# Slack instead of program order in the planner of a four-layer hybrid kernel

## The chip, the cores and the metric

The kernel runs on one core of a Trainium2 chip. The metric is device time in microseconds: before the change the median of three runs is 7542.12 us (7540.26 to 7549.51). Five engines work side by side, each through its own queue in order: TensorE (PE, matrix products), VectorE (DVE), ScalarE (ACT), GpSimd (POOL), and SyncE (SP), whose queue only starts transfers here. An instruction that isn't ready holds up everything behind it on its engine.

## The reference

The input `x` is 4 images of 96 channels, 64 by 64, in fp32. Four layers follow one another:

- Layer 0: two Mamba blocks over the 4096 pixels of an image as a sequence. In each: layer norm, a projection to 2 x 192 channels, a causal convolution of 4 taps, SiLU, and then a selective scan with 16 states per channel. Last a pooled gate, a 1x1 fusion, batch norm over all images, and the residual.
- Layer 1: group norm, then two 2-D selective-scan blocks ("ss2d"), each with a 3x3 depthwise convolution and a scan with 8 states in four directions (row by row, column by column, and both reversed), layer norm and a gate.
- Layer 2: a Fourier mixing layer over the tokens and a feed-forward layer quantized to a small float format.
- Layer 3: attention without softmax, and another such feed-forward layer.

The part that fills both planned stages is the scan:

```python
def step(h, inp):
    a, bu, c = inp                 # a = exp(delta * A), bu = delta * B * x
    h = a * h + bu
    return (h, jnp.einsum('bkdn,bkn->bkd', h, c))
```

## The kernel before

The kernel has three stages, one after the other: `stage_mamba` (layer 0), `stage_ss2d` (layer 1) and `stage_tokens` (layers 2 and 3). The third is written in the order in which it is issued. In the first two the code only records its operations, with a planner (`class Plan`, line 281), and `pl.run(tc)` at the stage's end issues them in the order that the planner chose. Every planned instruction carries line 466 in the profile, the line in `Plan.run` that issues it, so the profile's groups are told apart by tile names.

**The scan.** Both stages cut the sequence into turns of 1024 tokens. A turn is split into scan units: one unit is 128 rows (states times channels) by 1024 tokens. A mamba turn has 24 units and there are 32 turns; an ss2d turn has 6 units, and 128 turns make eight blocks of 96 units: 768 units in each stage. A block is one of the two ss2d layers on one image. For one unit:

- SP loads `sc_d`, the step `delta` spread over the states, from the DRAM tile `dd`; ACT turns it into the decay with Exp.
- In two units of three ("spread" units) PE makes `s`, `delta * x` spread over the rows, in PSUM (`Scan.inputs`), and DVE multiplies it by `B` (`bc`). In the third unit SP loads it as `sc_u` from `ud`, POOL multiplies it by `B`, and ACT writes the decay to `s`.
- DVE runs the scan (`TENSOR_TENSOR_SCAN`, 1024 steps); ACT copies the last column to `carry` for the next turn.
- POOL multiplies by `C` into `sc_h` (`Scan.outputs`), and PE sums over the states into `y` (`Scan.reduce`).

Besides, each turn has to be prepared: projections, convolution, `delta`, their way through DRAM (`dd`, `ud`, and in ss2d `bcd`, `bc_in` and `bc_stack` for `C`); and finished: gate, output projection. In ss2d a whole block is also convolved ahead (nine taps, 576 matmuls over the eight blocks, `mm<-xp,w_conv` in the profile) and normed behind. These side works are recorded between the units, step by step, by `Work.pace`; in ss2d the finish of the block before and the preparation of the block after are one such work, spread over the units of the running block (`between`, due near its end).

Buffers: `s` has two PSUM tiles, `y` one, `sc_d` six, `sc_u` three (two in ss2d), `sc_h` seven (five in ss2d). These are rings whose turn is fixed as the code is recorded. Only the two `mm` PSUM tiles are handed out by the planner itself (`Hold`).

**The planner.** `Plan.add` records an operation with a fixed cost from `Plan.cost` (its engine and its columns), and `Plan.touch` adds the operations it must come after. `Plan.order` (line 384) then plays the schedule forward. Every engine has a clock; the engine that can start first takes, among its ready operations, the one with the lowest `index`, the place in which the code recorded it. An engine never waits for a better operation while it has a ready one. Table switches on ACT cost `SWITCH`, a change of matmul form `TURN`, a hand-over between engines `SYNC`. An operation that needs an `mm` tile when none is left is parked; a freed tile wakes the one parked operation with the lowest index.

Of the kernel before, what the change touches and what calls it, by code (L numbers as in the profile page):

```python
# [280 lines left out]
class Plan:  # L281
# [2 lines left out]


    TABLE = {AF.Exp: "exp", AF.Silu: "silu", AF.Softplus: "softplus"}
    SWITCH, TURN, SYNC = 1283.0, 100.0, 100.0

    def __init__(self, nc):
        self.nc, self.ops, self.seen, self.open = nc, [], {}, None  # L290
# [91 lines left out]
        return 60.0  # L382

    def order(self):
        free = {}
        for hold in {h for op in self.ops for h in op.holds.values()}:

            first = hold.ops[0]
            first.after |= {by for op in hold.ops for by in op.after if by.index < first.index}
            for op in hold.ops[1:]:  # L390
                op.after.add(first)
        for op in self.ops:
            op.left = len(op.after)
            for by in op.after:
                by.then.append(op)
            for hold in op.holds.values():
                hold.left = len(hold.ops)
                free.setdefault(id(hold.ring), ([(0.0, t) for t in hold.ring], []))
        names = ("tensor", "vector", "scalar", "gpsimd", "sync")
        wait, can = {n: [] for n in names}, {n: [] for n in names}  # L400
        clock = dict.fromkeys(names, 0.0)
        table, form, link, out = None, None, 0.0, []
        for op in self.ops:
            if not op.left:
                heappush(wait[op.engine], (0.0, op.index, op))
        while len(out) < len(self.ops):
            at, name = min(
                (clock[n] if can[n] else max(clock[n], wait[n][0][0]), n) for n in names if can[n] or wait[n]
            )
            while wait[name] and wait[name][0][0] <= at:  # L410
                _, index, op = heappop(wait[name])
                heappush(can[name], (index, op))
            _, op = heappop(can[name])
            new = [h for h in op.holds.values() if h.buffer is None]
            if new:
                assert len(new) == 1
                buffers, parked = free[id(new[0].ring)]
                if not buffers:
                    heappush(parked, (op.index, op))
                    continue  # L420
                since = min(b[0] for b in buffers)
                if since > at:
                    heappush(wait[name], (since, op.index, op))
                    continue
                n = min(range(len(buffers)), key=lambda n: buffers[n][0])
                new[0].buffer = buffers.pop(n)[1]
            cost = op.cost
            if op.form:
                cost += self.TURN * (op.form != form)
                form = op.form  # L430
            if op.table and op.table != table:
                cost += self.SWITCH
                table = op.table
            op.start = at
            clock[name] = op.end = at + cost
            if name == "sync":
                link = max(link, at + 2200.0) + op.land - 2200.0
                op.end = link
            out.append(op)
            for hold in op.holds.values():  # L440
                hold.left -= 1
                if not hold.left:
                    buffers, parked = free[id(hold.ring)]
                    end = max(o.end for o in hold.ops) + self.SYNC
                    buffers.append((end, hold.buffer))
                    if parked:
                        _, o = heappop(parked)
                        heappush(wait[o.engine], (end, o.index, o))
            for o in op.then:
                o.ready = max(o.ready, op.end + (self.SYNC if o.engine != name else 0.0))  # L450
                o.left -= 1
                if not o.left:
                    heappush(wait[o.engine], (o.ready, o.index, o))
        return out

    def run(self, tc):
# [1229 lines left out]
```

## Time and profile before

| | |
|---|---|
| median of three runs | 7542.12 us |
| the profiled execution | 7571.38 us, span 7569.0 us |
| instructions | 84054 |
| PE, DVE, ACT, POOL busy over the span | 88%, 76%, 59%, 76% |
| mean clock granted to PE | 0.905 |
| scan on DVE, mean of one | 2.3 us (x1536) |
| multiply on POOL, mean of one | 2.36 us (x2048) |
| table loads on ACT | 499, 1283 ns each |
| HBM traffic | 1238.48 MB read, 174.06 MB written |

From the first scan to the last, mamba takes 72 to 2876 us and ss2d 2985 to 6170 us; the tokens stage begins at about 6230. A busy share is an average over a stage; what an engine waits for is in the lists of waits, where a line names the waiting engine and tile, what released it, and then total us, times, and the longest. A group's line has the busy time and the mean of one in ns, and after the second bar the idle time of the engine just before the group's instructions. Matmuls overlap and their ends are modelled, so that PE's busy time is not a measure of how much more it could do.

### The profile page before, as it was taken

The numbers are of one execution on the slowest core, as the hardware profiler recorded it, in microseconds if no ns is written. First come the engines' busy times: TensorE is split into PE (matmuls) and PEld (weight loads), VectorE is DVE, ScalarE is ACT, GpSimd is POOL, SyncE is SP. The second block draws the span as 40 slices with busy tenths as digits, with TensorE's granted clock in tenths as the row PEclk, the third lists the DMA queues.
The fourth block names the chain that finished last, engine by engine and source line by source line (L and its number), as shares of the span: only waits on it lengthen the run. The fifth ranks groups of instructions, "written<-read, shape, count | busy, mean of one in ns | idle before, by whom it ended". The sixth has DMA issues, their size and how long they took to land. (4 is left out here: it accounts for less than half of the span.)

```text
span 7569.0 us, 84054 instructions
## 1 busy us (share of the span) xinstructions
PE 6648.2 (88%) x28616; PEld 2867.8 (38%) x28616; DVE 5764.4 (76%) x4491; ACT 4499.9 (59%) x6656; POOL 5765.3 (76%) x2836
## 2 busy tenths in 40 slices
PE   8888888988888877989898898989898868999997
PEld 3322233323323222323232333323232228778784
DVE  6989988988898985898887878788888863344342
ACT  4655555555555544777777676677777644445442
POOL 6989988989998985889897978889898870232323
PEclk9999999999999998999898898989898888889897
DMA  7988988988888886999898989899999960000000
GB/s 192 239 224 232 230 216 220 239 222 226 227 235 217 222 224 168 233 241 230 223 234 222 244 218 241 215 230 232 230 238 238 236 176 22 1 18 5 15 9 9
DMA packets 448078, 1418.13 MB, mean 187 GB/s; under 512 B 81626, under 2 KB 91539, under 8 KB 445600
## 3 DMA queue, kind: packets, MB, share of 16 engines
q1 hardware_dynamic: 447648, 1412.76, 72.7%
q8 instruction: 225, 3.69, 0.2%
q14 instruction: 205, 1.68, 0.1%
HBM read 1238.48 MB, written 174.06 MB: 187 GB/s over the span
## 5 line engine op out<-in xcount | busy, mean ns | idle before, releaser
L466 POOL TENSOR_TENSOR sc_h<-sc_d,bc 128x1024 f32<-128x1024 f32 x1024 | 2406.9, 2360 | 394.8 <-DVE sc_d L466 186.0
L466 DVE TENSOR_TENSOR_SCAN sc_d<-sc_d,carry,s 128x1024 f32<-128x1024 f32 x768 | 1799.7, 2344 | 74.7 <-ACT sc_d L466 18.2
L466 DVE TENSOR_TENSOR s<-s,bc 128x1024 f32<-128x1024 f32 x1024 | 1248.7, 1220 | 505.3 <-PE s L466 500.2
L466 PE MATMUL s<-du,c_sel 96*128 96x512 f32 x2048 | 1124.0, 678 | 226.6 <-DVE sc_d L466 127.3
L466 ACT ACTIVATE sc_d<-sc_d,w_alog 128x1024 f32<-128x1024 f32 x1024 | 1165.7, 1144 | 257.4 <-DMA sc_d<-dd 253.7
L466 POOL TENSOR_TENSOR sc_h<-sc_u,bc 128x1024 f32<-128x1024 f32 x512 | 1208.0, 2359 | 112.2 <-PE y L466 73.1
L466 POOL TENSOR_TENSOR sc_u<-sc_u,bc 128x1024 f32<-128x1024 f32 x512 | 1208.2, 2360 | 100.9 <-DMA sc_u<-ud 87.6
L466 PE MATMUL y<-sc_h,c_red 128*32 128x512 f32 x6144 | 1094.5, 656 | 87.2 <-POOL sc_h L466 83.2
L466 DVE TENSOR_TENSOR_SCAN sc_u<-s,carry,sc_u 128x1024 f32<-128x1024 f32 x384 | 895.2, 2331 | 36.7 <-ACT s L466 17.5
L466 PE MATMUL s<-du,c_selp 128*128 128x512 f32 x1408 | 729.8, 647 | 112.3 <-DVE sc_d L466 108.8
L466 PEld LDWEIGHTS s<-du,c_sel 96*128 96x128 f32 x2048 | 396.2, 208 | 869.8 <-issue 427.7
L466 ACT ACTIVATE s<-sc_d,w_alog 128x1024 f32<-128x1024 f32 x512 | 570.8, 1115 | 240.7 <-DVE sc_d L466 155.7
L466 ACT ACT_TABLE_LOAD x499 | 640.2, 1283 | 8.7
L466 DVE TENSOR_TENSOR_SCAN sc_d<-sc_d,s 128x1024 f32<-128x1024 f32 x256 | 583.1, 2282 | 23.0 <-ACT sc_d L466 6.2
L508 POOL TENSOR_TENSOR ln_rs<-ln_rs_e,mhalf 128x4 f32<-128x4 f32 x128 | 134.9, 1056 | 582.9 <-DVE ln_rs_e L506 581.2
L466 PE MATMUL mm<-xp,w_conv 96*96 96x512 f32 x1152 | 528.7, 600 | 4.6 <-ACT bc L466 2.2
L466 PEld LDWEIGHTS y<-sc_h,c_red 128*32 128x32 f32 x6144 | 197.7, 114 | 848.9 <-issue 529.7
L466 ACT COPY carry<-sc_d 128x1 f32<-128x1 f32 x768 | 142.8, 186 | 565.5 <-DVE sc_d L466 564.0
L466 PEld LDWEIGHTS s<-du,c_selp 128*128 128x128 f32 x1408 | 263.2, 201 | 539.4 <-issue 274.7
L466 PE MATMUL mm<-hn,conv_w 97*64 97x512 f32 (+1 forms) x1024 | 368.8, 615 | 22.5 <-DVE hn L466 22.5
L466 PEld LDWEIGHTS mm<-xp,w_conv 96*96 96x96 f32 x1152 | 185.3, 164 | 310.1 <-issue 295.5
L466 DVE TENSOR_TENSOR_SCAN sc_u<-s,sc_u 128x1024 f32<-128x1024 f32 x128 | 290.7, 2271 | 14.1 <-ACT s L466 7.9
(211 smaller groups left out, 9343.6 us busy)
## 6 DMA issues: line engine op xcount, KB each, us to landing
sc_d<-dd SPq DMA_DIRECT2D x1536, 512.0 KB
sc_u<-ud SPq DMA_DIRECT2D x512, 512.0 KB
bc<-dd SPq DMA_DIRECT2D x128, 512.0 KB
dd<-delta SPq DMA_DIRECT2D x128, 448.0 KB
bc<-bcd SPq DMA_DIRECT2D x64, 512.0 KB
ud<-du SPq DMA_DIRECT2D x192, 128.0 KB
dd<-delta SPq DMA_DIRECT2D x32, 512.0 KB
ud<-du SPq DMA_DIRECT2D x32, 512.0 KB
```

Of the source, the lines that this page charges most:

```text
L466: getattr(getattr(self.nc, op.engine), method)(*a, **kw)
L508: nc.gpsimd.tensor_tensor(rs, ve, self.mhalf[:p, 0:n], ALU.pow)
```

## The change

The planner no longer ranks by `index` alone. It makes six rounds. In each it plays the schedule forward by the ranks it has (`schedule`, in the first round by `index`), notes the end that its own costs give, and then plays the schedule backward from that end (`push_back`): each engine takes the operations from the last to the first, those that ended latest first, as late as what follows them allows. An operation's start in this backward schedule, the latest that it found, becomes its rank for the next round, so that an operation with much slack ranks late. The round with the earliest end by the planner's costs is issued, with the `mm` tiles that it chose. A smaller change goes with it: a freed `mm` tile now wakes all operations parked for one, not only the first.

```diff
-    SWITCH, TURN, SYNC = 1283.0, 100.0, 100.0
+    SWITCH, TURN, SYNC, ROUNDS = 1283.0, 100.0, 100.0, 6
...
         for op in self.ops:
-            op.left = len(op.after)
+            op.rank = op.index
             for by in op.after:
                 by.then.append(op)
+        best = None
+        for _ in range(self.ROUNDS):
+            out = self.schedule()
+            end = max(op.end for op in out)
+            if best is None or end < best[0]:
+                best = end, out, {op: list(op.holds.values()) and [h.buffer for h in op.holds.values()] for op in out}
+            self.push_back(out, end)
+        for op in best[1]:
+            for h, buffer in zip(op.holds.values(), best[2][op] or ()):
+                h.buffer = buffer
+        return best[1]
+
+    def push_back(self, out, end):
+        names = ("tensor", "vector", "scalar", "gpsimd", "sync")
+        wait, can = {n: [] for n in names}, {n: [] for n in names}
+        clock = dict.fromkeys(names, 0.0)
+        for op in out:
+            op.left, op.ready = len(op.then), 0.0
+            op.length = op.end - op.start
+            if not op.left:
+                heappush(wait[op.engine], (0.0, -op.end, op.index, op))
+        for _ in out:
+            at, name = min(
+                (clock[n] if can[n] else max(clock[n], wait[n][0][0]), n) for n in names if can[n] or wait[n]
+            )
+            while wait[name] and wait[name][0][0] <= at:
+                _, rank, index, op = heappop(wait[name])
+                heappush(can[name], (rank, index, op))
+            _, _, op = heappop(can[name])
+            done = at + op.length
+            clock[name] = at + op.cost if name == "sync" else done
+            op.rank = end - done
+            for o in op.after:
+                o.ready = max(o.ready, done + (self.SYNC if o.engine != name else 0.0))
+                o.left -= 1
+                if not o.left:
+                    heappush(wait[o.engine], (o.ready, -o.end, o.index, o))
+
+    def schedule(self):
...
             if not op.left:
-                heappush(wait[op.engine], (0.0, op.index, op))
+                heappush(wait[op.engine], (0.0, op.rank, op.index, op))
...
                 if not buffers:
-                    heappush(parked, (op.index, op))
+                    parked.append(op)
                     continue
...
-                    if parked:
-                        _, o = heappop(parked)
-                        heappush(wait[o.engine], (end, o.index, o))
+                    for o in parked:
+                        heappush(wait[o.engine], (end, o.rank, o.index, o))
+                    parked.clear()
...
                 if not o.left:
-                    heappush(wait[o.engine], (o.ready, o.index, o))
+                    heappush(wait[o.engine], (o.ready, o.rank, o.index, o))
```

Nothing else changes: the recorded operations, their costs, the rings and the third stage are the same.

More of the change, by code (lines that the diff above doesn't have):

```diff
@@ L384, in order @@
     def order(self):
-        free = {}
         for hold in {h for op in self.ops for h in op.holds.values()}:
@@ L392, in order @@
         for op in self.ops:
-            op.left = len(op.after)
+            op.rank = op.index
             for by in op.after:
                 by.then.append(op)
+        best = None
[35 more added lines that the diff above has]
+    def schedule(self):
+        free = {}
+        for op in self.ops:
+            op.left, op.ready = len(op.after), 0.0
             for hold in op.holds.values():
-                hold.left = len(hold.ops)
+                hold.left, hold.buffer = len(hold.ops), None
                 free.setdefault(id(hold.ring), ([(0.0, t) for t in hold.ring], []))
@@ L410, in order @@
             while wait[name] and wait[name][0][0] <= at:
-                _, index, op = heappop(wait[name])
-                heappush(can[name], (index, op))
-            _, op = heappop(can[name])
+                _, rank, index, op = heappop(wait[name])
+                heappush(can[name], (rank, index, op))
+            _, _, op = heappop(can[name])
             new = [h for h in op.holds.values() if h.buffer is None]
@@ L418, in order @@
                 if not buffers:
-                    heappush(parked, (op.index, op))
+                    parked.append(op)
                     continue
-                since = min(b[0] for b in buffers)
-                if since > at:
-                    heappush(wait[name], (since, op.index, op))
+                buffers.sort(key=lambda b: b[0])
+                if buffers[0][0] > at:
+                    heappush(wait[name], (buffers[0][0], op.rank, op.index, op))
                     continue
-                n = min(range(len(buffers)), key=lambda n: buffers[n][0])
-                new[0].buffer = buffers.pop(n)[1]
+                new[0].buffer = buffers.pop(0)[1]
             cost = op.cost
```

## The prediction

> **What bounds the kernel now.** I read the page's 40 slices first, for stages; then busy times in windows, one for each stage and four of 100 us inside the second; then, in the worst of these, the groups of instructions and who waited for whom; last the same list of waits over the whole run.
>
> The slices. PE, DVE, POOL and the clock granted to PE, 189 us to a digit. DVE and POOL stand at 8 and 9 up to slice 33 and then drop: that end is the third stage, which has no planner.
>
> ```profile
> PE   8888888988888877989898898989898868999997
> ...
> DVE  6989988988898985898887878788888863344342
> ...
> POOL 6989988989998985889897978889898870232323
> PEclk9999999999999998999898898989898888889897
> ```
>
> Busy times by window: start:end, length, then PE, PE's weight loads, DVE, ACT and POOL, each with its count, then clock, DMA share and GB/s. The first three rows are the stages (mamba, ss2d, tokens).
>
> ```profile
> 0.00:2850.00 2850.00, 2494.04 (x8578) 848.55 (x8580) 2503.82 (x1588) 1588.87 (x2162) 2519.46 (x1113) 0.93 0.87 224
> 2850.00:6230.00 3380.00, 2921.96 (x8568) 1010.35 (x8564) 2777.36 (x1953) 2324.80 (x3459) 2894.77 (x1332) 0.90 0.88 225
> 6230.00:7569.00 1339.00, 1232.20 (x11473) 1008.93 (x11472) 483.21 (x952) 586.23 (x1035) 351.10 (x392) 0.86 0.05 14
> ```
>
> ```profile
> 4100.00:4200.00 100.00, 70.99 (x180) 20.92 (x182) 73.32 (x47) 60.21 (x94) 76.60 (x35) 0.78 0.85 213
> 4400.00:4500.00 100.00, 99.92 (x292) 34.75 (x291) 74.53 (x47) 69.00 (x97) 74.90 (x34) 1.00 0.74 195
> 4500.00:4600.00 100.00, 72.77 (x200) 22.29 (x200) 84.90 (x54) 80.58 (x118) 84.34 (x37) 0.88 0.98 254
> 4800.00:4900.00 100.00, 99.49 (x280) 34.24 (x279) 77.10 (x49) 70.69 (x102) 85.00 (x37) 1.00 0.83 221
> ```
>
> In both planned stages three engines share the load almost evenly: in mamba 88% each, in ss2d PE 86%, POOL 86%, DVE 82%. Neither stage has one bound; each loses what the three lose by being heavy at different times. In mamba they are heavy together. In ss2d they take turns: PE runs at 99% in one stretch and at 71 to 73% in the next, some 400 us apart, which is one block of 96 scan units. Inside 4400:4500:
>
> ```profile
> L466 PE MATMUL mm<-xp,w_conv 96*96 96x512 f32 x115 | 50.9, 594 | 0.0
> POOL sc_h L466 <- PE y L466: 19.2, 7, 4.6
> DVE s L466 <- PE s L466: 16.5, 8, 3.8
> ```
>
> Half of PE's time there is the convolution of the next block, never idle before it, while the scan's multiply on DVE waits for its `s` and POOL waits for `y`. Over the whole run:
>
> ```profile
> DVE s L466 <- PE s L466: 500.2, 311, 15.6
> POOL sc_h L466 <- DVE sc_d L466: 186.0, 153, 11.9
> ```
>
> The 500 us of DVE waiting for `s` is the largest wait of a well-loaded engine in the planned stages, and what an order can change.
>
> **What the Trainium skill says.** "Perfetto Trace Analysis", Optimization Strategy: a kernel with several regimes may gain by "interleaving those regimes". The windows above agree that ss2d has two. The same page, Identifying the Most-Contended Engine, warns that busy PE is not PE at its limit; the trace agrees (weight loads fill 30% of ss2d where matmuls fill 86%), so I weigh POOL and DVE as much as PE. "TensorE: Matmul & The Clock Gate", Architectural detail: ACT and DVE are strict FIFO; so an instruction that stands too early blocks all behind it. Its Part 1 has the clock halved after an idle window; here the clock is 0.78 where PE is 71% busy and 1.00 where it is 99.9%.
>
> **The change part by part.** No instruction of the planned work is added or removed; `order` at line 384 hands out the same operations in another order, with other buffers for the `mm` tiles. What follows is counted from the two kernels' orders as built.
>
> 1. It does act. In mamba the fourth of the six rounds is issued, in ss2d the second. Mean shift of an operation in its engine's queue: PE 12 and 14 places of 2,472 and 2,824, ACT 9 and 10, DVE 6 and 2, POOL 2 and 1.
>
> 2. PE's load in ss2d is spread. I counted the convolution's 576 matmuls between every 24 scan units: before, the eight blocks have pairs such as 63 then 9 or 51 then 21; after, 34 and 38, or 34 and 27. Then I gave every operation its mean from the trace's groups (scan 2.33, POOL multiply 2.36, DVE multiply 1.22, PE matmuls scaled so that ss2d sums to 2,919 us beside the trace's 2,922), put each engine's operations to the scan units they stand between, and summed over stretches the busiest engine's load. By 24 units: 3,229 us before, 3,101 after, minus 128 (in one block PE 128 then 78 before, 97 then 104 after, against POOL's 85). By 12 units minus 120; by 6 minus 98; by 8 minus 64; by 4 plus 8. Which length is right depends on how far engines drift apart: `s` has two buffers, `sc_h` five, loads run five units ahead, so 6 to 12. Bounds: plus 8 to minus 128; I take minus 80. A second way gives nearly that: mamba, whose PE load is even, needs 2,804 us from its first scan to its last for 2,535 us of POOL work; at this ratio ss2d's 2,817 us of POOL work in the same window take 3,116 us, 69 less than its 3,185.
>
> 3. The same sum in mamba changes by between plus 6 and minus 13 at 6 to 24 units. But there too the longest stretches of other PE work between two `s` shrink: those over 10 us fall from 24 to 11 (ss2d: 27 to 12), what lies beyond 8 us from 161 to 118 us. Bounds 0 and minus 43; DVE's queue and POOL's fill part of it, so I take minus 20.
>
> 4. Against it: PE changes between output heights 169 times more (1,014 to 1,104; 1,357 to 1,436). No row prices a change. From 0, since PE has some 10% idle, to 0.5 us each, the excess of a weight load's wait of 0.79 us after a change over the 0.24 us without one: 85 us. I take 10. Four more table loads at 1,283 ns are 5 us on ACT, which is 69% busy in ss2d: nothing, and 5 us without that cover.
>
> 5. Loads get later. SP is one queue in order, and it waits now (for POOL's `sc_h` alone, 1,705 us). I took for every load of `sc_d` the latest work that it or a DMA ahead of it in SP's queue waits for, and counted units from there to its own scan. In ss2d before, 4 loads have a lead of one unit or less and 11 of two; after, 18 and 32, behind the small `bcd` and `bc_in` transfers. Mamba hardly changes. A unit takes 4.15 us (3,185 us of scans over 768). The first load is issued at 64.5 us and its decay starts at 72.2: at most 7.7 us, then 1.15 us of decay. A lead of one is late by up to 4.7 us, of two by 0.6: 17 x 4.7 + 32 x 0.6 = 98, less the same sum of before, 21: 77 us at most. The start's 7.7 us has a queue of other loads in it, so I take 15.
>
> 6. The stages' ends: the last 8 units of ss2d stand in the same order, the 100 us between the stages and the drain at 6170:6230 keep their chains. Nothing; no cover is needed. The tokens stage is untouched.
>
> Sum: minus 80, minus 20, plus 10, plus 15: minus 75 us. The profiled execution took 7,571.4 us around a span of 7,569.0, 29 us above the median of 7,542.1; I take the difference from each alike: 7,496 profiled, 7,467 as median.
>
> **The rivals.** *Already absorbed.* The time of 24 scan units in ss2d is read from the starts of the scans: the stretch of the heaviest PE load (115) took 98 us and a light one (70) 112. Buffers carry some of the peak over, and the sum by 4 units says no gain. Then minus 40 to plus 15: 7,530. Against it: 16.5 and 19.2 us of waits in a single 100 us.
>
> *More than that.* If the flatter PE lets DVE's 500 us of waits fall by half, both stages gain: 7,290. For it: PE's clock sags in exactly the light stretches (0.78) and would do so less. Against it: the second way of part 2, which ends at minus 69 for ss2d.
>
> *Slower: late loads.* In ss2d's queue on SP a `bcd` write that waits for ACT stands ahead of the next `sc_d`; its decay comes late, the scan behind it holds DVE, and POOL starves. Price: the full 77 us of part 5, with part 4 at 85 us, against a gain of 100: 7,604. It decides from where the 49 late loads cost more than 100 / 49 = 2 us each. Against it: DVE waited for ACT's `sc_d` only 21 us in ss2d before. For it: POOL already waits 58 us there on loads of `sc_u`.
>
> *No change at all*, because the first round is issued, is excluded by part 1.
>
> **How the numbers follow.** The likeliest, minus 40 to minus 160 (7,382 to 7,502), has 0.54. More than that 0.13; absorbed 0.16, of which 0.07 within 0.2%, about what a measurement of this kernel can tell from no change, and 0.09 a little faster; late loads 0.17. Faster 0.54 + 0.13 + 0.09 = 0.76, same 0.07, slower 0.17. The range takes in the absorbed case, half of the late loads, and half of the large gain: 7,340 to 7,590.
>
> **What would show it.** Right: no stretch of ss2d with PE at 99% beside one at 72%; DVE's waits for `s` well under 500 us; from first scan to last some 3,110 us in ss2d (now 3,185) and 2,785 in mamba (now 2,804). Part 5 shows as ACT's waits for DMA before `sc_d`, now 254 us. Wrong: DVE's waits for `s` gone to ACT's decay, or the same length of ss2d with an even PE. The order was planned on fixed costs; where a real duration differs, a queue that stands tighter passes each delay on, and that could undo all of it.

## The result

The changed kernel takes 7565.74 us (median of 20 runs, 7542.01 to 7599.86) beside 7546.77 us before (20 runs, 7527.69 to 7566.74): ratio 1.0027, 95% interval 1.0015 to 1.0038. It is slower by some 20 us. The forecast was 75 us less; the time lies in the range, on the wrong side of no change.

The profiled execution took 7586.82 us around a span of 7585.0. The stages, from the starts of the scans in the two traces:

| us | before | after |
|---|---|---|
| mamba, first scan to last | 2802.8 | 2809.8 |
| last mamba scan to first ss2d scan | 109.3 | 105.5 |
| ss2d, first scan to last | 3183.8 | 3209.4 |
| last scan to the end | 1399.7 | 1384.9 |

So ss2d has the largest difference of this pair, 25.6 us, more than the 16.0 us between the two spans; mamba has 7.0 us more, and the last row, most of it the tokens stage in which nothing changed, has 14.8 us less. One execution of each is not enough to give ss2d's loss a size: the order of before took 3,184 us here and 3,167 in a kernel below, the changed one 3,209 here and 3,180 below. The verdict is that of the timed runs; the traces are read for what moved inside.

The page's slices after, PE, DVE, POOL and PE's clock, to be held against those of before:

```profile
PE   8899898988888987799989898889898777999997
...
DVE  6889988997999885887988788888888863344343
...
POOL 5989998998999885888998888889898961232323
PEclk9999999999999987898999899989899878889897
```

Busy times by window, as before: the first two stages, then the same four stretches of ss2d (start:end, length, then PE, weight loads, DVE, ACT, POOL, clock, DMA share, GB/s):

```profile
0.00:2850.00 2850.00, 2504.73 (x8555) 848.35 (x8558) 2494.16 (x1578) 1584.39 (x2157) 2511.03 (x1109) 0.92 0.87 223
2850.00:6230.00 3380.00, 2918.61 (x8491) 1012.42 (x8486) 2789.54 (x1930) 2330.73 (x3453) 2888.10 (x1323) 0.90 0.89 224
```

```profile
4100.00:4200.00 100.00, 85.33 (x235) 28.25 (x236) 81.69 (x55) 80.06 (x119) 82.04 (x36) 0.91 0.97 244
4400.00:4500.00 100.00, 97.76 (x277) 33.22 (x277) 90.50 (x57) 78.20 (x113) 86.18 (x38) 0.96 0.87 218
4500.00:4600.00 100.00, 89.17 (x250) 28.95 (x249) 80.78 (x51) 77.78 (x113) 82.00 (x36) 0.94 0.97 232
4800.00:4900.00 100.00, 95.70 (x281) 32.66 (x282) 88.17 (x55) 76.63 (x110) 89.13 (x39) 1.00 0.94 233
```

PE is even now: 85, 98, 89 and 96% where it was 71, 100, 73 and 99%. What the change was expected to do to PE it did, and the stage is no shorter.

The list of waits over the whole run, the line that was shown of before (there 500.2) and two that changed with it (before: 253.7 and 155.7):

```profile
DVE s L508 <- PE s L508: 439.0, 308, 10.5
...
ACT sc_d L508 <- DMA sc_d<-dd: 327.2, 239, 7.5
ACT s L508 <- DVE sc_d L508: 315.2, 145, 8.5
```

Now DVE's waits inside ss2d alone (2985 to 6170 us: total, times, longest), first before, then after:

```profile
DVE s L466 <- PE s L466: 289.0, 170, 15.6
DVE bc_in L466 <- ACT mm L466: 41.6, 33, 3.5
...
DVE sc_u L466 <- POOL sc_u L466: 22.0, 25, 2.7
DVE sc_d L466 <- ACT sc_d L466: 21.1, 13, 4.1
```

```profile
DVE s L508 <- PE s L508: 224.3, 155, 5.6
DVE sc_d L508 <- ACT sc_d L508: 62.0, 33, 6.5
DVE bc_in L508 <- ACT mm L508: 53.8, 55, 3.1
DVE sc_u L508 <- POOL sc_u L508: 36.1, 28, 5.8
```

The wait for `s` is 65 us less (15.6 of it is one wait ahead of the first scan of before). The waits for the decay, for a copy of ACT and for POOL's `sc_u` are 41, 12 and 14 us more. DVE waits as long as before, for others.

**Where in a turn.** I took the step from each scan's start to the next, and put DVE's busy and idle time into it. A turn of ss2d has six units, so by their places in DVE's queue 127 steps lead into the first unit of a turn and 640 stay inside one. (Busy and idle add up to some 50 us more than the steps, since records of neighbours overlap.)

| ss2d, us | into a turn: sum | busy | idle | inside: sum | busy | idle |
|---|---|---|---|---|---|---|
| before | 487.8 | 417.8 | 73.3 | 2696.0 | 2370.2 | 373.6 |
| after | 592.2 | 454.3 | 142.0 | 2617.3 | 2343.9 | 318.4 |

Inside the turns 79 us are gone, which looks like the 80 us of the prediction's part 2; into the turns 104 us have come. A third of the pair is no time at all but work that changed its place: of the 512 multiplies `s<-bc` 115 stand in the step into a turn where 87 did, and 28 x 1.22 us is 34 us. The rest is idle time: 55 us less inside, 69 us more at the turns' starts, where DVE's wait for the decay rose from 2 to 41 us and that for `s` from 56 to 78 (inside the turns the wait for `s` fell from 217 to 149).

One such start in the timeline of after (start, length, engine, instruction, idle time before it and what ended it):

```profile
4336.42 3.97 PE L508 MATMUL y<-sc_h,c_red 128*32 128x512 f32 x12
...
4340.32 0.60 PE L508 MATMUL mm<-bc_stack,selbc 24*128 24x512 bf16 x2
4340.74 1.07 ACT L508 COPY bc<-mm 128x512 f32<-128x512 f32 x2 [6.65 <-PE mm L508]
...
4341.83 1.28 ACT L508 ACT_TABLE_LOAD   x1
...
4343.12 2.19 ACT L508 ACTIVATE sc_d<-sc_d,w_alog 128x1024 f32<-128x1024 f32 x2
...
4344.31 2.35 DVE L508 TENSOR_TENSOR_SCAN sc_d<-sc_d,carry,s 128x1024 f32<-128x1024 f32 x1 [6.55 <-ACT sc_d L508]
```

ACT sits idle for 6.65 us with a copy at the head of its queue that needs PE's broadcast of `C`; PE makes this only after twelve `y` matmuls, which themselves wait for POOL's multiplies in between, and its weight load has a last wait of 0.84 us for a DMA. Then come the copies, a table load and only then the decay that the scan needs. DVE pays 6.55 us. Walking back through ACT's queue like this from every start of a turn, 8 of the 41 us end at the decay's own load, and the other 33 at an ACT instruction ahead of the decay, 32 of them one that waited for PE or DVE.

### The profile page after: what moved, and what is told of

It is laid out like the page before. It is cut to its first block, busy times and chain, and to the rows that moved or that the text cites. A ratio compares the mean times of both kernels' runs of the same rounds, so it can differ in the third digit from the quotient of the medians.

```text
span 7585.0 us, 84230 instructions
## 1 busy us (share of the span) xinstructions
PE 6668.7 (88%) x28616; PEld 2873.2 (38%) x28616; DVE 5777.9 (76%) x4491; ACT 4510.9 (59%) x6660; POOL 5763.7 (76%) x2836
## 5 line engine op out<-in xcount | busy, mean ns | idle before, releaser
L508 PE MATMUL s<-du,c_sel 96*128 96x512 f32 x2048 | 1104.8, 668 | 178.7 <-DVE sc_d L508 100.7
L508 PE MATMUL y<-sc_h,c_red 128*32 128x512 f32 x6144 | 1050.7, 644 | 62.7 <-POOL sc_h L508 54.1
L508 PE MATMUL s<-du,c_selp 128*128 128x512 f32 x1408 | 752.2, 665 | 159.4 <-DVE sc_d L508 154.6
L508 PE MATMUL mm<-xp,w_conv 96*96 96x512 f32 x1152 | 552.2, 609 | 6.8 <-DVE bc_in L508 3.0
L508 POOL TENSOR_TENSOR du<-delta,xc 96x1024 f32<-96x1024 f32 (+2 forms) x128 | 267.5, 2090 | 86.0 <-ACT delta L508 31.2
```

Source lines behind the costliest of these rows:

```text
L508: getattr(getattr(self.nc, op.engine), method)(*a, **kw)
```

## The experiments

Two questions: which part of the change makes the two shifts, and is either of them what part 2 and part 5 of the prediction said? And then, what does hold ss2d?

**The change in one stage only.** The old `order` is kept beside the new one, and one stage uses it (the first line stands in `stage_ss2d` in the first kernel, in `stage_mamba` in the second):

```diff
+    pl.slack = False
...
-            for op in self.order():
+            for op in (self.order() if self.slack else self.order_old()):
```

> Slack ranks in the mamba stage only; ss2d keeps the order of before. Late-first-units theory (in ss2d the even PE load gains some 80 us inside the turns and the first units of each turn lose some 100): mamba is neutral, 7540 to 7555 us, first scan to last within 10 us of 2803. Rival, the loss comes from mamba's order: 7560 to 7575.

> Slack ranks in ss2d only; mamba keeps the order of before. Late-first-units theory: all of the change is here, 7560 to 7580 us; steps from one turn's last scan to the next turn's first sum to about 590 us (488 before), all other steps to about 2617 (2696 before). Rival, loss from mamba: 7540 to 7550.

Measured: in mamba alone 7550.28 us, ratio 1.0003 (0.9991 to 1.0015), its scans 2,809 us; in ss2d alone 7544.16 us, ratio 0.9998 (0.9984 to 1.0013), its scans 3,180 us, 587.7 into the turns and 2592.3 inside. Neither stage gains. ss2d shows the two shifts again, as the late-first-units theory said, but not the 7560 to 7580 us that it gave. The two ratios do not add up to the 1.0027 of both; what is missing, 0.0026, is somewhat more than the three intervals together allow (about 0.0022), and nothing here explains it.

**More buffers for `sc_d`,** re-planned, in the changed kernel and in the one before:

```diff
-    sc = Scan(k, rep, ps, NS1, k.load(wp, "c_red1"), (6, 2, 5))
+    sc = Scan(k, rep, ps, NS1, k.load(wp, "c_red1"), (8, 2, 5))
```

> The changed kernel with eight sc_d buffers in ss2d instead of six, so that a load no longer waits for the late sc_h of the unit six before. Late-first-units theory: the steps between turns fall from 592 to under 520 us, the others stay near 2617, so about 7480 to 7500 us. Rival, the slower clock of PE (half clock for 771 us of ss2d against 665): buffers do not touch it, 7555 to 7575. Rival, a load is late because its turn is prepared late: also no change, 7555 to 7575.

> The kernel before with eight sc_d buffers in ss2d. Late-first-units theory: its steps between turns (488 us for 127, 3.84 each) are already as short as the rest, so little: 7525 to 7550 us. Rival, more buffers help any order alike: as much less than before as the changed kernel with eight buffers is less than the changed kernel.

Measured: changed 7615.21 us, ratio 1.0088 (1.0070 to 1.0107), 459.9 into the turns and 2783.0 inside; before with eight tiles 7534.36 us, ratio 0.9977 (0.9967 to 0.9987), 465.1 and 2706.9. The planner makes another order for other buffers, so this compares two orders, not two buffer counts: the starts of the turns became short as expected, and the steps inside lost more. (The 771 and 665 us of half clock in the first expectation are not of like windows: between the first and the last scan of ss2d they are 608 us after and 577 before.) The kernel before with eight tiles is the one version with the whole computation that is clearly below both kernels.

**The same order, more tiles.** To keep the order, the tile is exchanged only as the instruction is issued, with a deeper ring for the `sc_d` of the spread units, six tiles where there were four:

```diff
+                u.swap = {u.d.tensor.name: self.deep[self.count % self.ahead]}
...
+    sc.ahead = 6
```

> The changed kernel, every queue in its order; the spread units of ss2d take their sc_d tile from a ring of six instead of four (the other units keep their two), so that the load of a unit waits for the sc_h of nine units before, not of six. This replaces the earlier exchange, in which one ring of eight let a load overwrite a tile whose scan was still to come. Late-first-units theory, link 2 (a late sc_h holds the tile, and so the next turn's load): steps between turns 592 to about 490 us, others near 2617, 7455 to 7485 us. Rival (late by place in SP's queue, by landing or by ACT's queue): steps between turns over 560, 7550 to 7575.

> The same exchange under the order of before. Late-first-units theory: steps between turns stay within 25 of 488 us; 7525 to 7550 us. Rival, more tiles help any order: the same gain as the changed kernel has from it.

Measured: changed 7559.05 us, ratio 1.0020 (1.0008 to 1.0032), 588.5 into the turns and 2614.3 inside; before 7539.65 us, ratio 0.9990 (0.9980 to 1.0000), 480.1 and 2681.4. The loss at the turns' starts stays to within 4 us: it is not that a late multiply by `C` holds the tile for the next load.

An earlier form of this had one ring of eight for all units:

> The changed kernel with every queue's order kept instruction by instruction; only the tile behind each ss2d unit's sc_d is changed as it is issued, from a ring of six to a ring of eight. Late-first-units theory: a load at a turn's start then waits for the sc_h of the unit eight before, not of the late one six before: steps between turns 592 to about 490 us, all others stay near 2617, so about 7455 to 7485 us. Rival, these loads are late by their place in SP's queue or by their landing: steps between turns stay over 560, 7550 to 7575 us.

> The same exchange of tiles under the order of before. Late-first-units theory: little to gain, its steps between turns are short already: 7525 to 7550 us. Rival, eight tiles help any order: as much less as the changed kernel loses.

Measured: 8086.43 us and 7991.65 us, ratios 1.0698 and 1.0581. A load could now come to stand ahead of the scan that had to read its tile, so POOL waited 331.8 us for loads of `sc_d` in the changed order; both orders lose alike, and it tells nothing of the question.

**Without the way of `C`.** POOL multiplies by `B`, which arrives by DMA, in place of `C`, one row of `bc` ahead of it (the output is another one):

```diff
+                return bass.AP(v.tensor, v.offset - T, v.ap)
```

> The changed kernel, every queue in its order; in ss2d POOL multiplies by the table of B instead of that of C, which is still made and copied, so that sc_h no longer waits for the chain that brings C (bc_in, bc_part, bcd, bc_stack, mm, bc). The sum over states is then taken with B for C. Late-first-units theory, link 1 (the first sc_h of a turn waits for C): POOL's 61 us of waits for ACT's bc go, steps between turns 592 to under 520, 7470 to 7500 us. Rival, POOL has other work first or SP's order is the cause: over 560, 7550 to 7575.

> The same under the order of before, B for C in ss2d's sum over states. Late-first-units theory: POOL's 91 us of waits for ACT's bc go here too, but the turns' first units were in time: 7520 to 7547 us, steps between turns within 25 of 488. Rival: as much gain as in the changed kernel.

Measured: 8023.30 and 8015.95 us, ratios 1.0628 and 1.0615. POOL waited some 550 us for loads of `bc` in both orders: the load of a later turn's `B` was not planned around multiplies that still read the one before. It can't say what `C` costs.

**Waking all without slack, slack without waking all.** The diff has two parts. The first kernel keeps the waking of all operations parked for an `mm` tile, with one round, so that the rank is the index; the second keeps six rounds of slack and wakes one:

```diff
-    SWITCH, TURN, SYNC, ROUNDS = 1283.0, 100.0, 100.0, 6
+    SWITCH, TURN, SYNC, ROUNDS = 1283.0, 100.0, 100.0, 1
```

```diff
-                    parked.append(op)
+                    heappush(parked, (op.rank, op.index, op))
...
-                    for o in parked:
-                        heappush(wait[o.engine], (end, o.rank, o.index, o))
-                    parked.clear()
+                    if parked:
+                        _, _, o = heappop(parked)
+                        heappush(wait[o.engine], (end, o.rank, o.index, o))
```

> One round: ranks by index as before, and only the smaller part of the change, that a freed mm tile wakes all parked operations. It moves nothing in mamba. If the ranks make the first units late: 7540 to 7560 us, steps between turns within 30 us of 488. Rival, the waking does it: steps between turns over 560, the other steps still near 2690, over 7600 us.

> Slack ranks and six rounds as in the change, but a freed buffer wakes one parked operation, as before it. In ss2d this order spreads the convolution's matmuls (at most 44 of a block's 72 in 24 scan units, where before has 72 and the change 41), but the first units of turns keep their early loads: 4 of 768 loads lead their scan by two units or less, as in before (3; the change 11). If the spread of PE's load is what saved the 79 us inside the turns, and the waking of all what cost the 104 us at their starts, ss2d keeps the gain and loses the cost: starts of turns near 490 us, all other steps near 2,615, together 3,105 against 3,184, and the time is near 7,470. If spreading PE's load is worth nothing, and both the gain inside and the loss at the starts come from the waking of all (the order that has that alone, with the convolution as bunched as before, showed 591 and 2,584), the other steps stay near 2,690, and the time is 7,530 to 7,560.

Measured: waking alone 7556.75 us, ratio 1.0007 (0.9992 to 1.0022); slack alone 7579.96 us, ratio 1.0047 (1.0031 to 1.0062).

| ss2d | convolution matmuls in its fullest stretch of 24 scans, after the first block | into a turn | inside | all |
|---|---|---|---|---|
| before | 62 | 487.8 | 2696.0 | 3183.8 |
| waking all, no slack | 61.5 | 590.8 | 2584.1 | 3174.9 |
| slack, waking one | 44 | 506.8 | 2697.1 | 3203.9 |
| the change | 41 | 592.2 | 2617.3 | 3209.4 |

(The matmuls are counted in the traces, two records for one. The first block's 72 stand in one stretch in all four orders; the 72 of the second expectation is that.) Of the first expectation no branch came whole: the starts are those of its rival, the time is that of the other, and the 2,584 us inside are in neither. Of the second, the steps inside came as its last sentence has them, and the time came longer.

This is the result that decides. The order whose convolution is as bunched as before has both shifts; the order that spreads the convolution has neither the gain inside nor much of the loss. So the 79 us that seemed to confirm part 2 come from the small change of the diff, which I had not priced at all. The clock granted in ss2d does not make the difference: it is 0.93 with waking alone, but 0.90 to 0.91 in the other three rows, and 0.91 with the change in ss2d alone, which has 2592.3 us inside. The two shifts look like one shift in phase, the first unit of a turn later behind its preparation and the next five closer behind it; that is a reading of the sums. The starts are not even late for the same waits: with waking alone DVE waits there 51 us for a copy of ACT to `bc_in` (15 before, 5 in the change) and 26 for decays (41 in the change).

What the slack itself does is the third row against the first: the fullest stretch goes from 62 to 44, and ss2d is no shorter. Nor is the wait that the spread should have shortened. DVE's wait for `s` in ss2d, 289.0 us before, with waking alone and then with slack alone:

```profile
DVE s L508 <- PE s L508: 198.8, 140, 4.0
```

```profile
DVE s L508 <- PE s L508: 264.9, 171, 6.7
```

Inside the turns it is 217 us before, 135 with waking alone and 214 with slack alone. That other effects of the slack cancel some gain of the spread is not excluded, but there is no sign of such a gain in this wait.

**What PE's load is worth.** Both orders, with eight of nine matmuls of each group of the convolution left out as they are issued (the output is another one):

```diff
+                    if op.engine == "tensor" and a[1].tensor.name.startswith("w_conv1"):
+                        if not kw["start"]:
+                            continue
+                        kw = dict(kw, stop=True)
```

> The order of before with eight of the nine matmuls of each group of the second stage's convolution left out (470 us of PE's 2,922 us there; the output is another one). This bounds what any order of the convolution can gain. If its bunching is what holds ss2d, as part 2 has it, the time falls by 100 us or more, to below 7,450. If buffers absorb the bunches, it falls by less than 50 us.

> The same matmuls left out in the order of the change. If the spread is why the change loses nothing inside the turns, there is less left to win here than in before: it ends later than before without them by the loss at the turns' starts alone, some 100 us. If the spread is worth nothing, it ends within 40 us of before without them.

Measured: 7595.04 us in the order of before, ratio 1.0060 (1.0040 to 1.0080), ss2d 3,242 us; 7604.56 us in the changed order, ratio 1.0071 (1.0047 to 1.0094), ss2d 3,237 us. The steps are 497.7 and 2743.9 in the first, 598.1 and 2639.3 in the second: the two shifts are there with hardly any convolution, and the two kernels end 10 us apart, as expected if the spread is worth nothing. That both would be slower than before, with 470 us of matmuls less on PE, neither theory had. The groups of `s` on PE and DVE within ss2d, before and then without the convolution (busy us, mean ns, idle time before):

```profile
L466 PE MATMUL s<-du,c_sel 96*128 96x512 f32 x2044 | 1122.1, 679 | 226.6 <-DVE sc_d L466 127.3 <-DVE sc_u L466 72.5 <-DVE ln_rs_e L466 15.9
...
L466 DVE TENSOR_TENSOR s<-s,bc 128x1024 f32<-128x1024 f32 x512 | 624.8, 1221 | 291.9 <-PE s L466 289.0 <-DMA sc_u<-ud 1.6 <-DMA ud<-du 0.5
```

```profile
L470 PE MATMUL s<-du,c_sel 96*128 96x512 f32 x2008 | 1216.3, 740 | 372.3 <-DVE sc_d L470 247.9 <-DVE sc_u L470 102.2 <-DVE ln_rs_e L470 13.6
...
L470 DVE TENSOR_TENSOR s<-s,bc 128x1024 f32<-128x1024 f32 x502 | 612.9, 1221 | 299.4 <-PE s L470 298.4
```

With less in its queue PE sits idle before `s` for 372 us, 350 of them waiting for DVE's scans, which free the two `s` tiles; and DVE still waits 298 us for `s`. The two wait for each other in turns. I read that wait as the length of a way (the scan ends, PE makes `s` in two matmuls of the code, which are four records of 512 columns, DVE multiplies), not as a queue on PE; halving `s` below puts it to the test. The clock granted in ss2d fell from 0.91 to 0.83 and a matmul of `s` grew from 679 to 740 ns, so the way became longer. "TensorE: Matmul & The Clock Gate", Part 1, of the Trainium skill has the clock halved when PE has been idle; the direction agrees. That the clock is the whole of the 58 us is an inference.

**ACT's queue.** The changed order; 186 of 512 decays of ss2d are moved ahead by one to seven places on ACT:

```diff
+            ready = max((by.start + 7500.0 for by in op.after if by.engine == "sync"), default=0.0)
...
+                if prev in op.after or prev.table or at[prev] <= low or prev.start < ready:
+                    break
+                act[m] = prev
```

> The order of the change, in which 186 of the 512 decays of ss2d are moved ahead on ACT by one to seven places, past copies and casts, wherever their load was planned to be issued 7.5 us earlier. If DVE's 41 us of waits for decays at the turns' starts are ACT's queue (a decay behind a copy that waits for PE), most of it goes: ss2d 30 us shorter, ratio to the change 0.996, to before near 0.999. If the loads are late themselves, the waits turn from the copy to the DMA, and the time stays at 7,565; if the copies that are passed are what POOL and DVE need next, it is longer.

Measured: 7706.65 us, ratio 1.0211 (1.0190 to 1.0232), ss2d 3,345 us. ACT's waits for a load ahead of a decay, and DVE's for the cast that was passed (139.1 and 53.8 us in after):

```profile
ACT sc_d L529 <- DMA sc_d<-dd: 214.3, 135, 8.7
```

```profile
DVE bc_in L529 <- ACT mm L529: 126.0, 70, 7.1
DVE sc_d L529 <- ACT sc_d L529: 47.1, 22, 6.1
```

DVE's waits for decays fell by 15 us, its waits for the passed casts rose by 72. ACT's waits for loads rose by 75. The second and the third outcome came true together, at a size that I had not expected: moving one engine's instructions by a few places cost 120 us of the profiled span. So this way of moving decays ahead on ACT costs more than it gives; another one is not excluded.

**What holds ss2d, then?** Three halves in the order of before, one at a time: the loads of `sc_d`, the matmuls of `s`, POOL's multiplies by `C` (the outputs are others). The lines are excerpts of the edits, in this order:

```diff
+                        kw["out"], kw["in_"] = half(kw["out"], 0), half(kw["in_"], 0)
```

```diff
+                    if late:
+                        if n:
+                            continue
```

```diff
+                        a = [half(v) for v in a]
```

> The order of before; in ss2d each load of an sc_d tile brings the first 512 of its 1,024 columns, and each decay is made by two activations of 512 columns that both read these (the output is another one; ACT does 768 more activations of about half the length). The DMA moves some 200 MB less of 734 MB in ss2d, where its packets fill 90% of the 16 engines' time. If the transfers are what holds ss2d (the loads come 7.4 us and more after their issue, and every buffer turns over at that pace), its scans take under 3,050 us, and the time is below 7,420. If they are hidden, and DVE, POOL and PE hold it by waiting for each other, they stay at 3,140 to 3,200.

> The order of before; in ss2d the second of the two matmuls of each s is left out from the 13th on (the output is another one), which halves the way from the scan that frees an s buffer, over PE, to DVE's multiply. If DVE's 289 us of waits for s in ss2d are that way's length and not PE's load elsewhere (leaving out 470 us of convolution made them longer), they fall to below 170, and ss2d by 60 us or more. If they are set by something else, they stay above 230 and ss2d within 30 us of 3,184.

> The order of before; in ss2d POOL's multiplies by C take 512 of 1,024 columns from the 13th on (the output is another one), some 1.2 us less each for 768 of them, 900 us of POOL's 2,895. If POOL's load holds ss2d, it falls by 200 us or more, to below 2,980, until DVE's 2,790 us stop it. If the transfers hold it, it falls by less than 60 us: SP's waits for sc_h end earlier, but no tile arrives sooner.

Measured: half the loads 7547.04 us, ratio 0.9998 (0.9985 to 1.0012), ss2d 3,172; half of `s` 7509.10 us, ratio 0.9952 (0.9933 to 0.9971), ss2d 3,135; half of POOL's multiplies 7554.27 us, ratio 1.0011 (1.0001 to 1.0021), ss2d 3,189. The windows of ss2d, first before, then the three in this order, and below them DVE's wait for `s` with half of `s`:

```profile
2985.00:6170.00 3185.00, 2786.57 (x8173) 954.46 (x8171) 2703.10 (x1830) 2252.31 (x3364) 2817.03 (x1281) 0.91 0.91 230
```

```profile
2985.00:6170.00 3185.00, 2777.49 (x8188) 951.81 (x8187) 2702.00 (x1829) 2442.84 (x4127) 2815.21 (x1281) 0.92 0.59 168
```

```profile
2985.00:6170.00 3185.00, 2602.56 (x7316) 819.46 (x7314) 2705.81 (x1859) 2255.11 (x3377) 2825.57 (x1296) 0.84 0.91 231
```

```profile
2985.00:6170.00 3185.00, 2764.84 (x8166) 951.91 (x8167) 2691.70 (x1826) 2246.96 (x3363) 2007.65 (x1279) 0.90 0.91 230
```

```profile
DVE s L475 <- PE s L475: 152.1, 100, 5.0
```

The DMA share falls from 0.91 to 0.59 and the time stays. (ACT carries 191 us more for it, as two activations stand for one; that this ate a gain is not excluded, but ACT is at 77%.) POOL's busy time falls by 809 us and the time stays, where 200 us or more were expected if POOL's load held ss2d. The way over `s`, halved, is the only one of the three with a gain: 49 us of ss2d in this pair, 36 us in the timed runs, though PE's clock falls to 0.84, about as far as without the convolution. DVE's waits for `s` are 137 us shorter, and others of DVE (for `y`, for `mm`) take up part. Of the expectation the wait came (152.1, below 170), the 60 us did not quite.

So in ss2d neither PE's convolution, nor POOL's multiplies, nor the transfers set the time in this order, each taken alone; that two of them hold it together was not tried. What remains is DVE's own work, 2,703 us of the 3,185 of the window, with its short waits, of which the one over `s` is the largest. DVE's work was not halved, so it is what is left over, not shown.

## Why the prediction was wrong

*The bound.* "Each loses what the three lose by being heavy at different times" is the sentence that failed first. It was read from busy shares that are nearly equal, in ss2d 86, 86 and 82%. Taking work away shows that they do not mean the same: POOL could lose 809 us and PE 470 us of matmuls with no gain.

*Part 1, the change acts:* right, as far as the order goes, but the count took both parts of the diff together, and I priced only the slack. The waking of all moves the turns' starts by 103 us alone.

*Part 2, minus 80 for the spread of PE's load:* the spread came (85 to 98% in the four stretches), and the step that gave it a value failed: to sum over stretches the busiest engine's load. That sum prices a queue on PE which is not there: leaving the convolution out makes ss2d 58 us longer, and the order that spreads it without waking all has 2,697 us inside the turns beside 2,696 before, where minus 80 was forecast, and is the slower one at 1.0047. (The lower clock without the convolution may hide a gain; the second of these has no such flaw, its clock in ss2d is 0.905 where it was 0.909.) The second way, mamba's time over POOL's work, agreed by chance: halving POOL's multiplies gave nothing. The 79 us found inside the turns have another cause. "Perfetto Trace Analysis", Optimization Strategy, of the Trainium skill says that performance "may be improved by interleaving those regimes"; here the regimes were evened out, and the time did not follow: the busier engine in them, PE, was not one whose load, taken alone, set it.

*Part 3, minus 20 in mamba:* nothing came (2,803 and 2,810 us; mamba alone 1.0003). DVE's waits for `s` in mamba are 203 and 205 us. The long stretches of other PE work that the order removed were not what those waits consisted of.

*Part 4:* the four table loads are there (503), at no visible price. The price of height changes was not tried by itself.

*Part 5, later loads, plus 15:* the place was right, the starts of the turns behind the small transfers of `C`. The size was not: DVE's waits for decays in ss2d are 41 us more, 39 of them at the turns' starts. And the mechanism was half right: by the walk back through the queue the load itself has 8 of the 41 us there and ACT's queue 33. The sign that I had named came, ACT's waits for `sc_d` loads, 254 to 327 us, 49 of the 73 in ss2d; but little of it reached DVE. My count of short leads was off too: it put decays to a later unit than their own, and found 50 leads of two units or less; a count by the unit whose scan needs the load gives 11, and 3 before. Both hang on how units are counted and are no more than a sign of the direction. (The sum takes 17 and 3 loads with a lead of one where its text has 18 and 4; the difference is nearly the same.)

*Part 6, the ends:* as said; the tokens stage, in which nothing changed, differs by 15 us between the two executions.

*The rivals.* "Already absorbed" named the mechanism that the runs show, that the peaks hardly reached the scan, from the right view: the stretch of 24 units with the heaviest PE load was quicker than a light one. Its upper end, plus 15, would be plus 41 with part 5 at its measured 41 us; the timed runs say plus 20. I gave it 0.16. "Late loads" ended on the right side, but its cause has only 8 of the 41 us at the starts, and more tiles for the loads left the starts as they were. Both signs that I had named for being wrong came: DVE's waits for `s` went in good part to ACT's decay, and ss2d is no shorter with an even PE.

What stays open, first, is why the change is slower at all. Its 20 executions were granted a mean clock of 0.905, the 155 of before on record 0.910, and a line through these 155 gives 7,567 us at 0.905, which is the mean of the 20. So the loss goes along with a lower clock, as one execution of before differs from another; whether the clock is the cause, or only follows from PE waiting more, no run here shows. (Slack alone lies on the same line to 2 us; waking alone lies 20 us above it, at 0.913.) Open are also why slack in both stages is slower than in either alone; why slack without the waking is the slowest of the four (its waits for decays and for `sc_u` are 31 and 23 us above before, but one execution's scans scatter by nearly that); and whether DVE's own work is the bound.

## What to carry over

A wait of one engine for another says whose result is late, not that the other has too much to do: look whether the other was itself idle before it, as PE was before `s`, and leave that load out once before planning to move it. A diff of two parts wants each part priced and run alone, since an effect of the expected size can come from the other. And a forecast made of fixed costs can be too fine for the kernel: the planner saw 63 us of gain over its first round (26 in mamba, 37 in ss2d), while its six rounds for ss2d alone differ by 69, and the chip kept none of it. Here, where tiles go round with one or two buffers, a new order traded one short wait for another.

## What the runs showed of the hardware

- With less work on PE, other work on PE was slower: 470 us of matmuls fewer, the granted clock in ss2d 0.83 for 0.91, the matmuls of `s` 740 ns for 679, those of `y` 702 for 655.
- Over 155 executions of the kernel before, on five chips, the time goes with the clock granted over the run: 0.904 to 0.916, correlation -0.81, 41 us less for 0.01 more. A longer run may have more idle time and for that a lower clock, so this shows no direction.
- From the issue of a 512 KB load of `sc_d` to the start of its decay it took about 7.5 us in ss2d at the first percentile (lowest 6.7 to 6.9) and 13 in the median, before and after, with the decay's own wait in ACT's queue in it. The planner prices the landing at 4.3 us (2,200 ns and 512 KB at 250 bytes per ns).
